# Layers 2 and 3 of a four-layer graph network: TensorE bound to the order of the text, adjacency checks placed behind a chunk's products

## The chip, the cores and the metric

The kernel runs on one core of a Trainium2 chip. The core has five engines that run side by side and wait for one another through semaphores: TensorE (PE in the profile: matrix products and transposes), VectorE (DVE), ScalarE (ACT), GpSimd (POOL) and SyncE (SP, which here only issues transfers). The metric is the time of one execution in microseconds (us) on the device.

## The reference, cut to what matters

Input is x with 8 batches of 2048 nodes and 64 features, and an adjacency matrix of 2048 x 2048 zeros and ones. Four layers follow, each of the form x + layer(relu(layernorm(x))). The change touches the last two.

```python
# layer 2: three steps
v = causal_vars.at[:, intervention_idx].set(intervention_value)
for _ in range(MAX_STEPS):
    effects = jnp.einsum('nm,bmd->bnd', adj_matrix, v)
    h = jnp.concatenate([v, effects], axis=-1)
    h = jax.nn.relu(jnp.einsum('bnk,dk->bnd', h, W1) + b1)
    v = jnp.einsum('bnk,dk->bnd', h, W2) + b2
# layer 3: x, A x and (2 A A - I) x, each with its own weights for every node
w = jnp.einsum('nd,dkio->nkio', embedding, weight)
...
x_g = jnp.einsum('knm,bmc->bnkc', A_stack, x)
out = jnp.einsum('bnki,nkio->bno', x_g, w)
```

The large work is the product of the adjacency matrix with a 2048 x 128 matrix: three times in layer 2 and twice in layer 3, for each pair of batches.

## The kernel before, in words

The function `layers23` (L1438 to L1618) works on one pair of batches at a time (p = 0 to 3), so that 2 x 64 features fill the 128 partitions. The 2048 nodes are cut into 4 chunks of 512 columns (c = 0 to 3) and 16 tiles of 128 (m). The adjacency matrix stays in SBUF as 16 tiles aT.

A "spread" (`spread`, L1510) is one chunk of the product with the adjacency matrix: 32 matmuls of 128x512, two for each m, since the other factor is held as a rounded part `hi` and a rest `lo`. The two parts of a chunk of y are needed by every spread at its four values of m: the last chunk's by m = 12 to 15.

For a pair p the stages are:

- Entering (`enter`, L1519): load a chunk of x2, layer norm (`mean`, `xc`, square, `var`, Ln, Exp, `v`; `kit.norm_steps`, L720), then `moved`: four products `py` with W1e, and from them `hi` (ACT) and `lo`.
- Steps 0, 1 and 2 of layer 2 (L1538): for each chunk a product of v with W1v or Wvc (L1543, called Wv below), a spread, Relu into v (L1545). In steps 0 and 1 `moved` follows: `py` with Wec, `yb` (DVE, L1494), `hi` (ACT, L1495), `lo` (POOL, L1496). In step 2 instead: `pv` with W2 (L1550), `xq` on DVE, the bias sum `bq` on POOL, a store to x3, layer norm, and `turned`: four transposes `tp`, `hi`, `lo`.
- First product of layer 3 (L1565): four spreads into y1, each followed by `turned`.
- Second product and output (L1570): for each chunk a spread into y2, then four blocks of 128 nodes, each with a transpose `px` of x3, its copy `xs` on ACT, twelve products `u` for each half w of the weights (24 in all as the trace counts them), in pairs that use the two halves of the array, DVE's multiplication by the embedding (`pr`) and sums (`fold`), POOL's sums (`ot`) and the store of `out`. The next pair's chunk c - 1 enters at the start of chunk c; its chunk 3 enters after the loop (L1617).

The adjacency matrix must be checked for values other than 0 and 1: `check` (L1461) loads 64 pieces `raw` of 128x512, two ahead of each chunk as written, and DVE counts in each (L1470).

The program is written for a scheduler that orders each engine's instructions by what it expects to be ready; each engine then runs its list in that order. `tc.keep_in_program_order` binds an instruction to the order of the text. Before, only the `u` products are bound, except the first of each twelve:

```python
if kk or h:
    tc.keep_in_program_order(one)
```

Buffers come from pools; tiles of one tag share a number of buffers. `hi` and `lo` have 6 each, so that eight pairs of them can't be held at once; `raw` shares the two buffers of the tag "fold"; `tp`, `py`, `pv`, `px`, `mean` and `var` share two PSUM buffers.

Of the kernel before, what the change touches and what calls it, by code (L numbers as in the profile page):

```python
# [8 lines left out]
FP = mybir.dt.float32  # L9
FR = mybir.dt.float32r  # L10
AF = mybir.ActivationFunctionType
OP = mybir.AluOpType
# [4 lines left out]
P = 128  # L17
B, N, F = 8, 2048, 64
E = 64
NP = B // 2  # L20
NT = N // P
CW = 512
NCW = N // CW
# [8 lines left out]
def cols(c, w=CW):  # L32
    return slice(c * w, (c + 1) * w)
# [588 lines left out]
class Kit:  # L622
# [88 lines left out]
    def mm(self, *args, **kw):  # L711

        one = self.nc.tensor.matmul(*args, **kw)  # L713
        if self.strict:
            self.tc.keep_in_program_order(one)

# [718 lines left out]
        l1.close()  # L1435


def layers23(kit, aT, x2_dram, x3_dram, out):  # L1438

    tc, nc, t = kit.tc, kit.nc, kit.t  # L1440
    mm = nc.tensor.matmul
    ident, ones = kit.ident, kit.ones
    ctx = ExitStack()
    W1v, W1e, W2, Wvc, Wec, cb = kit.W1v, kit.W1e, kit.W2, kit.Wvc, kit.Wec, kit.cb
    b1, b2c, ivc, b1c = kit.b1, kit.b2c, kit.ivc, kit.b1c
    K3, D3 = 3, 16

    fin = ctx.enter_context(tc.tile_pool(name="f_in", bufs=2, reuse_waits="tile"))
    w2 = ctx.enter_context(tc.tile_pool(name="w2f", bufs=1, reuse_waits="tile"))
    sb = ctx.enter_context(tc.tile_pool(name="f_sb", bufs=2, reuse_waits="tile"))  # L1450
    ps = ctx.enter_context(tc.tile_pool(name="f_ps", bufs=2, space=PSUM, reuse_waits="tile"))

    def norm(dst, src):

        mean = ps.tile([P, CW], FP, tag="tp", name="mean")
        var = ps.tile([P, CW], FP, tag="tp", name="var")
        xc = fin.tile([P, CW], FP, tag="ca", name="xc")
        q = fin.tile([P, CW], FP, tag="q", name="q", bufs=1)
        kit.norm(dst, src, mean, var, xc, q)

    def check(n):  # L1461

        for _ in range(n):
            if not todo:
                return
            m, h = todo.pop(0)
            a = sb.tile([P, CW], FP, tag="fold", name="raw")
            nc.sync.dma_start(out=a, in_=t["adjT"][m * P : (m + 1) * P, cols(h)])
            k = 7 + NCW * m + h
            nc.vector.scalar_tensor_tensor(  # L1470
                a, a, 0.5, a, op0=OP.is_gt, op1=OP.not_equal, accum_out=kit.bad[:, k : k + 1]
            )

    todo = [(m, h) for m in range(NT) for h in range(NCW)]

    def parts():
        return (
            sb.tile([P, 4, P], FR, tag="hi", name="hi", bufs=6),
            sb.tile([P, 4, P], FR, tag="lo", name="lo", bufs=6),
        )  # L1480

    def moved(v, c, W, bias):

        py = ps.tile([P, 4, P], FP, tag="tp", name="py")
        for k in range(4):
            m = 4 * c + k
            mm(py[:, k, :], v[:, m * P : (m + 1) * P], W, start=True, stop=True)  # L1487
        hi, lo = parts()
        if bias is None:
            nc.scalar.copy(hi, py)  # L1490
            nc.vector.tensor_tensor(lo, py, hi.bitcast(FP), op=OP.subtract)  # L1491
        else:
            yb = fin.tile([P, 4, P], FP, tag="ca", name="yb")
            nc.vector.tensor_tensor(yb, py, bias[:, None, :].to_broadcast([P, 4, P]), op=OP.add)  # L1494
            nc.scalar.copy(hi, yb)  # L1495
            nc.gpsimd.tensor_tensor(lo, yb, hi.bitcast(FP), op=OP.subtract)  # L1496
        return hi, lo

    def turned(v, c):

        tp = ps.tile([P, 4, P], FP, tag="tp", name="tp")
        for k in range(4):
            m = 4 * c + k
            nc.tensor.transpose(tp[:, k, :], v[:, m * P : (m + 1) * P], ident)
        hi, lo = parts()
        nc.scalar.copy(hi, tp)  # L1506
        nc.vector.tensor_tensor(lo, tp, hi.bitcast(FP), op=OP.subtract)  # L1507
        return hi, lo

    def spread(acc, y, c, start):  # L1510

        for m in range(NT):
            for part in y[m // 4]:
                mm(acc, part[:, m % 4, :], aT[m][:, cols(c)], start=start, stop=m == NT - 1 and part is y[m // 4][1])  # L1514
                start = False

    v = fin.tile([P, N], FP, name="v", bufs=1)

    def enter(p, c):  # L1519

        xp = fin.tile([P, CW], FP, tag="x", name="xp")
        nc.sync.dma_start(out=xp, in_=x2_dram[p, :, cols(c)])
        norm(v[:, cols(c)], xp)
        if c == 0:
            nc.vector.tensor_copy(v[:, 0:1], ivc)
        return moved(v, c, W1e, None)

    y = [enter(0, c) for c in range(NCW)]
    W3 = w2.tile([P, K3, D3 * F], FP, name="W3f")
    for h in range(2):  # L1530
        nc.sync.dma_start(out=W3[half(h)], in_=t["L3_gnn_weight"])
# [2 lines left out]

    nc.vector.tensor_sub(W3[:, 0, :], W3[:, 0, :], W3[:, 2, :])
    nc.vector.tensor_scalar(W3[:, 2, :], W3[:, 2, :], 2.0, None, op0=OP.mult)
    for p in range(NP):
        for step in range(3):  # L1538
            yn = []
            for c in range(NCW):  # L1540
                acc = ps.tile([P, CW], FP, tag="acc", name="acc")
                check(2)
                mm(acc, Wvc if step else W1v, v[:, cols(c)], start=True, stop=False)  # L1543
                spread(acc, y, c, False)
                nc.scalar.activation(v[:, cols(c)], acc, AF.Relu, bias=b1c if step else b1)  # L1545
                if step < 2:
                    yn.append(moved(v, c, Wec, cb))
                    continue
                pv = ps.tile([P, CW], FP, tag="tp", name="pv")
                mm(pv, W2, v[:, cols(c)], start=True, stop=True)  # L1550
                xp = fin.tile([P, CW], FP, tag="x", name="xq")
                nc.sync.dma_start(out=xp, in_=x2_dram[p, :, cols(c)])
                nc.vector.scalar_tensor_tensor(xp, pv, b2c, xp, op0=OP.add, op1=OP.add)
                bq = sb.tile([P, CW], FP, tag="pr", name="bq", bufs=3)
                nc.sync.dma_start(out=bq, in_=kit.bias_dram[:, cols(c)])
                nc.gpsimd.tensor_add(bq, bq, xp)
                nc.sync.dma_start(out=x3_dram[p, :, cols(c)], in_=bq)
                norm(v[:, cols(c)], xp)
                yn.append(turned(v, c))
            y = yn  # L1560


        y1 = sb.tile([P, N], FP, tag="y1", name="y1", bufs=1)
        yn, after = [], []
        for c in range(NCW):  # L1565
            acc = ps.tile([P, CW], FP, tag="acc", name="acc")
            spread(acc, y, c, True)
            nc.scalar.copy(y1[:, cols(c)], acc)
            yn.append(turned(y1, c))
        for c in range(NCW):  # L1570
            acc = ps.tile([P, CW], FP, tag="acc", name="acc")
            spread(acc, yn, c, True)
            y2 = fin.tile([P, CW], FP, tag="ca", name="y2")
            nc.scalar.copy(y2, acc)
            xp = fin.tile([P, CW], FP, tag="x", name="xr")
            nc.sync.dma_start(out=xp, in_=x3_dram[p, :, cols(c)])
            if c > 0 and p + 1 < NP:
                after.append(enter(p + 1, c - 1))
            for k in range(4):
                i = 4 * c + k  # L1580
                ns, ks = slice(i * P, (i + 1) * P), slice(k * P, (k + 1) * P)
                px = ps.tile([P, P], FP, tag="tp", name="px")
                nc.tensor.transpose(px, xp[:, ks], ident)
                xs = sb.tile([P, 2, F], FP, tag="xs", name="xs", bufs=1)
                nc.scalar.copy(xs.rearrange("p h f -> p (h f)"), px)
                pr = []
                for w in range(2):
                    u = [ps.tile([P, 8, F], FP, tag=f"u{h}", name=f"u{h}") for h in range(2)]
                    for kk, src in enumerate((v[:, ns], y1[:, ns], y2[:, ks])):
                        for h in range(2):  # L1590

                            one = mm(  # L1592
                                u[h].rearrange("p d o -> p (d o)"), src[half(h), :], W3[half(h), kk, cols(w)],
                                start=kk == 0, stop=kk == 2,
                            )
                            if kk or h:
                                tc.keep_in_program_order(one)
                    for h in range(2):
                        a = sb.tile([P, 8, F], FP, tag="pr", name="pr", bufs=3)
                        nc.vector.tensor_tensor(  # L1600
# [2 lines left out]
                        if w:  # L1603
                            nc.vector.tensor_add(pr[h], pr[h], a)  # L1604
                        else:
                            pr.append(a)
                fold = sb.tile([P, 2, 4, F], FP, tag="fold", name="fold")
                ot = sb.tile([P, 2, F], FP, tag="ot", name="ot", bufs=1)
                for h in range(2):
# [4 lines left out]
                nc.sync.dma_start(  # L1614
                    out=out[2 * p : 2 * p + 2, ns, :].rearrange("h p f -> p h f"), in_=ot
                )
        y = after + [enter(p + 1, NCW - 1)] if p + 1 < NP else None  # L1617
    ctx.close()  # L1618


# [99 lines left out]
```

## Time and profile before

| | |
|---|---|
| time of three runs | 2155.81, 2156.43, 2158.01 us (median 2156.43) |
| span of the profiled execution | 2160.7 us |
| busy: TensorE, VectorE, ScalarE, GpSimd | 2056.3, 1211.0, 461.1, 297.4 us |
| spread matmuls (L1514) | 960 + 960 + 320 + 320 |
| products `u` (L1592) | 1024 + 512 |
| loads `raw` | 64 of 256 KB, 3.2 us from issue to landing (median) |

A line of the groups has the source line, the engine, the operation, output and inputs by their names in the program, and busy and mean times. The timeline has the start, the length, then the same, and in brackets how long the engine stood idle before and what ended it. The busy time of TensorE counts overlapping matmuls as they lie: spread matmuls last 0.4 us each in the records and start 0.23 us apart.

### The profile page before, as it was taken

The page shows a single profiled execution, that of the slowest core. Times are in us where ns is not written, and L with a number is a line of the kernel's source. Part 1 is how long each engine was busy: PE and PEld are TensorE (multiplying, and loading weights), DVE is VectorE, ACT ScalarE, POOL GpSimd, SP SyncE. Part 2 cuts the span into 40 slices and gives each one's busy share as a digit, 9 for nine tenths or more (in the row PEclk, how much of TensorE's full clock was granted, in tenths as well). Part 3 has the DMA queues.
Part 4 walks back from the last instruction along what each step waited for, and adds up shares of the span by engine and source line. Part 5 has one row for each costly group of instructions (what it writes and reads, how often), then busy time and mean ns, then how long its engine had stood idle before and what let it go on. Part 6 is the DMA issues. An engine that isn't in the chain of part 4 may idle for free.

```text
span 2160.7 us, 23805 instructions
## 1 busy us (share of the span) xinstructions
PE 2056.3 (95%) x9164; PEld 1156.7 (54%) x9164; DVE 1211.0 (56%) x1882; ACT 461.1 (21%) x860; POOL 297.4 (14%) x416
## 2 busy tenths in 40 slices
PE   7999889978999999989999999999999999999997
PEld 4777655523323232226775456665467754576653
DVE  6676488858898988874114652126550246401255
ACT  4322244456111111112121011210111210112100
POOL 0211154411000000000101211102111012111022
PEclk9999899989999999999999999999999999999999
DMA  5666362155011111015100022100030000101000
GB/s 124 182 185 192 104 226 51 37 163 173 28 55 44 54 44 50 30 58 144 35 30 15 24 74 79 35 10 25 21 106 12 33 15 23 37 1 34 12 19 12
DMA packets 86154, 140.26 MB, mean 65 GB/s; under 512 B 33040, under 2 KB 33296, under 8 KB 83792
## 3 DMA queue, kind: packets, MB, share of 16 engines
q1 hardware_dynamic: 67984, 88.05, 13.9%
q0 software_dynamic: 18048, 50.60, 7.8%
q8 instruction: 74, 1.21, 0.2%
q14 instruction: 48, 0.39, 0.1%
HBM read 107.89 MB, written 30.74 MB: 64 GB/s over the span
## 4 chain that ended last, share of the span: by engine, by line
PE 61%; issue 16%; DVE 8%; DMA 6%; POOL 4%; ACT 3%; POOLq 0%; DVEq 0%; SPq 0%; ACTq 0%
PE acc L1514 19%; PE o L713 10%; PE u L1592 7%; PE dn L713 5%; DMA raw<-in_adjT 3%; PE acc L919 2%; PE var L713 2%; PE pgs L1147 2%; PE py L1487 2%; PE mean L713 2%; PE acc L1543 1%; DVE pt L1375 1%; DMA at<-in_adjT 1%; DVE ex L1145 1%; POOL fold L1611 1%
## 5 line engine op out<-in xcount | busy, mean ns | idle before, releaser
L1514 PE MATMUL acc<-aT,hi 128*128 128x512 f32 x960 | 401.4, 418 | 0.0
L1514 PE MATMUL acc<-aT,lo 128*128 128x512 f32 x960 | 388.3, 405 | 0.0
L1592 PE MATMUL u<-W3f,y 64*128 64x512 f32 x1024 | 258.2, 592 | 0.0
L1375 DVE SCALAR_TENSOR_TENSOR pt<-R,wd,aT 128x1024 f32<-128x1024 f32 x192 | 236.9, 1279 | 22.9 <-PE dn L713 10.5
L713 PE MATMUL o<-pt,hS 128*64 128x512 f32 x1024 | 243.5, 602 | 5.7 <-DVE pt L1375 5.2
L1600 DVE TENSOR_TENSOR pr<-u,embf 128x512 f32<-128x512 f32 x256 | 171.4, 688 | 123.0 <-PE u L1592 110.6
L1514 PEld LDWEIGHTS acc<-aT,hi 128*128 128x128 f32 x960 | 180.8, 188 | 62.0 <-issue 23.2
L1514 PEld LDWEIGHTS acc<-aT,lo 128*128 128x128 f32 x960 | 180.7, 188 | 51.2 <-issue 13.6
L1592 PEld LDWEIGHTS u<-W3f,y 64*128 64x128 f32 x1024 | 104.2, 187 | 124.8 <-issue 124.8
L713 PEld LDWEIGHTS o<-pt,hS 128*64 128x64 f32 x1024 | 70.3, 137 | 169.8 <-issue 149.0
L1592 PE MATMUL u<-W3f,v 64*128 64x512 f32 x512 | 146.4, 617 | 0.0
L919 PE MATMUL acc<-at,Y 128*128 128x512 f32 x512 | 134.0, 406 | 1.9 <-DVE ev L928 1.9
L1514 PE MATMUL acc<-aTl,lo 128*128 128x512 f32 x320 | 129.0, 404 | 5.4 <-DVE lo L1491 4.0
L1514 PE MATMUL acc<-aTl,hi 128*128 128x512 f32 x320 | 128.4, 402 | 5.9 <-ACT hi L1495 5.9
L713 PE MATMUL dn<-pt,vd 128*32 128x512 f32 x1024 | 125.3, 598 | 2.7 <-DVE pt L1375 2.7
L1611 POOL TENSOR_TENSOR fold<-fold 128x256 f32<-128x256 f32 x64 | 46.9, 733 | 556.2 <-DVE fold L1610 556.2
L1494 DVE TENSOR_TENSOR yb<-py,cb_f 128x512 f32<-128x512 f32 x32 | 22.1, 690 | 158.2 <-PE py L1487 158.2
L919 PEld LDWEIGHTS acc<-at,Y 128*128 128x128 f32 x512 | 93.5, 191 | 24.3 <-issue 4.2
L1470 DVE SCALAR_TENSOR_TENSOR raw<-raw 128x512 f32<-128x512 f32 x64 | 49.9, 785 | 72.1 <-DMA raw<-in_adjT 71.7
L1604 DVE TENSOR_TENSOR pr<-pr 128x512 f32<-128x512 f32 x128 | 88.1, 688 | 2.2
L1507 DVE TENSOR_TENSOR lo<-tp,hi 128x512 fp32r<-128x512 f32 x32 | 22.1, 692 | 117.5 <-ACT hi L1506 117.5
L1375 DVE SCALAR_TENSOR_TENSOR pt<-R,wd,aTl 128x1024 f32<-128x1024 f32 x64 | 80.0, 1282 | 10.3 <-PE dn L713 7.4
(277 smaller groups left out, 2681.0 us busy)
## 6 DMA issues: line engine op xcount, KB each, us to landing
at<-in_adjT POOLq DMA_DIRECT2D x32, 512.0 KB, 4.7
raw<-in_adjT SPq DMA_DIRECT2D x64, 256.0 KB, 3.2
aT<-in_adjT POOLq DMA_DIRECT2D x12, 1024.0 KB, 6.4
R<-r_dram SPq DMA_DIRECT2D x14, 512.0 KB, 3.7
hi_dram<-hi SPq DMA_DIRECT2D x16, 264.0 KB, 2.6
lo_dram<-lo SPq DMA_DIRECT2D x16, 264.0 KB, 3.5
hhi<-hi_dram POOLq DMA_DIRECT2D x16, 264.0 KB, 3.1
hlo<-lo_dram POOLq DMA_DIRECT2D x16, 264.0 KB, 3.1
```

Source lines behind the costliest of these rows:

```text
L713: one = self.nc.tensor.matmul(*args, **kw)
L919: mm(acc[p], Y[h][:, m, p, :], at[:, k, :], start=m + h == 0, stop=m == NT - 1 and h == 1)
L1147: return lambda: mm(flat(pg), S[:, k, :], flat(mix), start=k == 0, stop=k == NB - 1)
L1375: nc.vector.scalar_tensor_tensor(pt, R[b2], wd[:, m, b2 : b2 + 1], aT[m][:, s].bitcast(FP), op0=OP.max, op1=OP.mult)
L1470: nc.vector.scalar_tensor_tensor(a, a, 0.5, a, op0=OP.is_gt, op1=OP.not_equal, accum_out=kit.bad[:, k : k + 1])
L1487: mm(py[:, k, :], v[:, m * P : (m + 1) * P], W, start=True, stop=True)
L1494: nc.vector.tensor_tensor(yb, py, bias[:, None, :].to_broadcast([P, 4, P]), op=OP.add)
L1514: mm(acc, part[:, m % 4, :], aT[m][:, cols(c)], start=start, stop=m == NT - 1 and part is y[m // 4][1])
L1592: one = mm(u[h].rearrange("p d o -> p (d o)"), src[half(h), :], W3[half(h), kk, cols(w)], start=kk == 0, stop=kk == 2,)
L1600: nc.vector.tensor_tensor(a, u[h], emb[:, i, 8 * w : 8 * w + 8, None].to_broadcast([P, 8, F]), op=OP.mult)
L1604: nc.vector.tensor_add(pr[h], pr[h], a)
L1611: nc.gpsimd.tensor_add(fold[:, :, 0:2, :], fold[:, :, 0:2, :], fold[:, :, 2:4, :])
```

## The change

Layers 2 and 3 are rewritten so that the order of TensorE's instructions is that of the text. All its products and transposes go through `kit.mm` and a new `kit.turn`, which bind them while `kit.strict` is set. So that other chunks' products can still come between, a small class `Weave` keeps a clock in the text: every emitted product adds a stated time (0.47 us for two spread matmuls, 0.93 for Wv, 2.8 for twelve `u`), and each chain of dependent steps is a generator that yields the time until its next product.

```diff
+    def passed(self, us):
+
+        self.now += us
+        for c in list(self.chains):
+            if c[0] <= self.now:
+                self.step(c)
...
+    def carry(c, step, yn):
+        yield 1.4
+        yn[c] = moved(v, c, Wec, cb, None if step else LENT[c])
...
+    def leave(p, c, xp, yn):
+
+        yield 1.4
+        pv = ps.tile([P, CW], FP, tag="tp", name="pv")
...
+        yield 1.8
+        yield from normed(v[:, cols(c)], xp, ("u0", "u1"))
+        yn[c] = turned(v, c, LENT[c])
```

The checks' loads are issued per chunk into the tag "x" (two buffers, shared with the chunks of x), and the counting is bound behind the chunk's spread in the text:

```diff
+                if step < 2:
+                    got = raw(2)
...
                 nc.scalar.activation(v[:, cols(c)], acc, AF.Relu, bias=b1c if step else b1)
                 if step < 2:
-                    yn.append(moved(v, c, Wec, cb))
-                    continue
...
+                    check(got)
+                weave.start(carry(c, step, yn) if step < 2 else leave(p, c, xp, yn))
```

`lo` is computed on DVE, not on POOL. Chunks 2 and 3 of step 0 and step 2 take their `hi` and `lo` from buffers lent by the tags "fold" and "pr". The layer norm uses v itself in place of the buffer `q`, and PSUM buffers of the tags "u0", "u1" or "acc" for `mean` and `var`. The first two chunks of layer 3's first product are interleaved. All four chunks of pair 0 enter before the first spread; chunks 2 and 3 are loaded into `room`, a tile in the place of y1. The entering of a later pair goes on between groups of twelve `u`, and its chunk 3 now enters during the output of chunk 3, in columns of y1, and is copied to v by ACT at the end:

```diff
+                weave.start(enter(c - 1, after, xp, 0.0, ("acc", "acc")))
+                if c == LAST:
+
+                    xp = load(y1[:, cols(0)], x2_dram[p + 1], c)
+                    weave.start(enter(c, after, xp, 2.0, ("acc", "acc"), y1))
...
+        two = [ps.tile([P, CW], FP, tag="acc", name="acc") for c in range(2)]
+        for ms in (range(0, 8), range(8, 12), range(12, NT)):
+            for c in range(2):
+                spread(two[c], y, c, 0 in ms, ms)
...
-        y = after + [enter(p + 1, NCW - 1)] if p + 1 < NP else None
+        if p + 1 < NP:
+            weave.until(lambda: None not in after)
+            nc.scalar.copy(v[:, cols(LAST)], y1[:, cols(1)])
+        y = after
```

## Prediction

> **What bounds the kernel now.** I read the page's totals first, then the times by stage, the waits of TensorE in layers 2 and 3, and the timeline where they fall.
>
> ```profile
> span 2160.7 us, 23805 instructions
> PE 2056.3 (95%) x9164; PEld 1156.7 (54%) x9164; DVE 1211.0 (56%) x1882; ACT 461.1 (21%) x860; POOL 297.4 (14%) x416
> ```
>
> TensorE (PE) is the only engine near full. Layers 2 and 3 run from 957 us to the end. The next view cuts them at the first product of step 0 of each batch pair p = 0, 1, 2, 3; the last stretch ends with the last `u` product.
>
> ```profile
> 957.45:970.97 13.52, 6.49 (x15) 3.34 (x15) 5.12 (x6) 6.19 (x8) 0.53 (x1) 0.62 0.28 88
> 970.97:1274.96 303.99, 297.71 (x1257) 185.66 (x1256) 123.79 (x222) 49.35 (x88) 39.93 (x57) 0.99 0.18 48
> 1274.96:1576.09 301.13, 292.78 (x1233) 183.14 (x1232) 120.68 (x218) 44.38 (x80) 41.87 (x60) 0.99 0.15 42
> 1576.09:1872.59 296.50, 291.42 (x1233) 182.86 (x1232) 115.34 (x203) 44.39 (x80) 41.99 (x60) 0.99 0.12 36
> 1872.59:2149.00 276.41, 275.67 (x1195) 176.18 (x1193) 95.16 (x158) 36.53 (x68) 41.62 (x60) 1.00 0.07 19
> ```
>
> First column is length, second PE's busy time. Pair 3 is 20 to 28 us shorter than the others. Two things are missing in it: the adjacency checks (done by 1617 us) and the entering of a next pair. They are what the change rearranges. Where PE waits:
>
> ```profile
> PE var L713 <- ACT q L727: 10.0, 14, 4.7
> PE acc L1514 <- ACT hi L1495: 5.9, 2, 3.6
> PE acc L1514 <- DVE lo L1491: 4.0, 2, 2.5
> PE acc L1514 <- POOL lo L1496: 1.4, 2, 0.9
> ```
>
> The last three are 11.3 us, in four places (1023, 1284, 1323, 1585 us). The DVE timeline at the third shows why:
>
> ```profile
> 1320.92 0.69 DVE L1470 SCALAR_TENSOR_TENSOR raw<-raw 128x512 f32<-128x512 f32 x1 [2.59 <-DMA raw<-in_adjT]
> ...
> 1325.09 0.69 DVE L1470 SCALAR_TENSOR_TENSOR raw<-raw 128x512 f32<-128x512 f32 x1 [2.44 <-DMA raw<-in_adjT]
> 1325.70 0.08 DVE L1470 DVE_READ_ACCUMULATOR raw<-raw 128x1 f32 x1
> 1325.70 0.69 DVE L1494 TENSOR_TENSOR yb<-py,cb_f 128x512 f32<-128x512 f32 x1
> ```
>
> `py` was finished at 1317.7, but `yb` stands behind three checks, each waiting for its load. `hi`, `lo` and TensorE wait behind `yb`; after that the spread products start 0.43 us apart instead of 0.23. The other loss is in the entering of a next pair, in layer 3 (PE timeline):
>
> ```profile
> 1176.46 1.02 PE L713 MATMUL mean<-xp,avg_f 128*128 128x512 f32 x2
> 1177.41 1.13 PE L1592 MATMUL u<-W3f,v 64*128 64x512 f32 x4
> 1178.92 1.13 PE L713 MATMUL var<-q,avg_f 128*128 128x512 f32 x2 [0.38 <-ACT q L727]
> 1179.98 1.98 PE L1592 MATMUL u<-W3f,y 64*128 64x512 f32 x6
> 1182.40 1.16 PE L1487 MATMUL py<-W1e_f,v 128*128 128x128 f32 x8 [0.44 <-DVE v L1525]
> ```
>
> `var` and `py` come too soon after what they need and wait 0.4 us each. Six `u` records are an odd three products: the pair of halves that otherwise start together (24 records in 5.35 us) is torn.
>
> [...] 8 us of delay for `yb`, ready all the time. [...] 0.43 us spacing after the 3.6 us wait, none after the 2.1 us at 1284. [...] `lo` is 1.29 us on POOL (L1496), 0.69 on DVE (L1491).
>
> **The change, part by part**, from the order in which the changed program issues on each engine; layers 0 and 1 keep theirs.
>
> *Checks.* Two per chunk in steps 0 and 1, on DVE directly before that chunk's `yb`, from two `x` buffers loaded a chunk ahead. The round is two checks (1.6 us), the issues and 3.2 us to landing (9.4 at worst once): under 6 us in a chunk of 9.4. So the four gaps go. Worth, from the stretches: the chunk at 1018.45 took 14.5 us instead of 9.45 (5.0); the one at 1317 6.6 too much; 1284.26 to 1286.81 2.1 too much; 1585.39 to 1592.94 4.4. Sum 18.1; it agrees with 11.3 us of waits and about 6.8 us of slow products. The DVE work per chunk (two checks, `yb`, `lo` from POOL: 3 us) lies beside 9.4 us of PE.
>
> *Entering in layer 3.* Chunks 1 to 3 take 27.59, 27.41 and 27.41 us with an entering, a chunk of pair 3 without takes 22.38. 82.4 - 67.1 = 15.3 us per pair; the products themselves (`mean` 0.95, `var` 0.97, `py` 1.0) need 2.9 x 3 = 8.8. In the new order they stand between whole groups of twelve `u`: `var` 5.35 us after `mean`, `py` 5.6 us after `var`. DVE has xc before the group, v before the fold: Exp is ready about 2.5 us after `var`, v at some 4. No wait, so 6.5 us per pair return: 19.5 for three.
>
> *Chunk 3 carries two enterings*, the second in `y1`'s columns; its 2.9 us of products come from step 0's first chunks, where they are now: no gain. A new wait: the second `py` needs the PSUM buffer of the first, which DVE's `lo` frees late, since v of the second waits for Exp, behind `xs`, behind POOL's `ot`. Counting on: `lo` ends 20.6 us into the chunk, PE is there at 19.3. Loss 1.4 per pair, 4.2 in all (bounds 0 and 10).
>
> *SP's queue in layer 3.* The loads of the entering stand between the stores of `out`, which wait for POOL's `ot` (some 6 us behind the last `u` of a block of rows). Each load is issued before the last store of its chunk, and the next chunk's 7.5 us of spreads cover the 3 us to landing: nothing. The load into `y1` waits for chunk 0's `u` only, two chunks ahead of its use: nothing.
>
> *First product of layer 3.* `tp` of the last chunk stands two spread products (0.47 us) ahead of the products that read it; `hi` ends 1.34 and `lo` 2.06 us after `tp` begins (trace at 1113). Before, 18 products lay between. Loss 0.9 x 4 = 3.6 (0.5 to 1.5 each).
>
> *Steps 0 to 2.* `py` and `pv` come two spread products after `Wv`. Today they come directly after it and wait for Relu (chunk 9.46). Apart they cost one more change from fp32 to fp32r, 0.40 us (0.63 against 0.23 after a 512-wide fp32 product). A chunk then is 7.47 + 0.86 + 1.06 = 9.39, the last step's 11.6 against 11.76. Gain 2, bounds -5 and +5. `lo` on DVE, lent buffers, ACT's three copies of 0.6 us: off PE's path; nothing, hidden under spreads.
>
> *Start of layer 2.* All four enterings now come before the first spread. On SP, chunks 2 and 3 (`room`) are behind two raw loads, which wait for xc of chunks 0 and 1 (961.1 and 961.8); W3f follows, held to 968.4 by layer 1's last store as today. DVE has the W3f subtraction before v of chunk 3; both loads land 6.1 to 8.2 us after issue, so 977, subtraction 1.2, v 0.7, `py` 1 to 2: first product at 981 instead of 970.97. But today's first chunks then hold three enterings (8.8 us and 0.4 of waits). Plus a slow clock in the first spreads: loss 1 (bounds: gain 4 if W3f lands early, loss 5).
>
> Sum against the span: 18.1 + 19.5 - 4.2 - 3.6 + 2 - 1 = 30.8. The profiled span, 2160.7, is 4.3 above the median 2156.43 of the runs: 2156.4 - 30.8 = **2125.6 us**.
>
> **Rivals.** (A) The bound order stalls in the entering: at 9 places v or Exp arrives 2 us late behind folds and POOL. For it: ACT's `xs` waits 302 us in all for POOL's `ot`. Against: v stands early in DVE's order. The 19.5 us vanish: 2145. (B) The start is better than I count and the new waits are absorbed: 30.8 + 5 + 4.2 + 3.6 = 44 us, 2113. (C) Slower: TensorE, no longer free to take another product, waits at each of the 48 `py`/`pv` behind Relu. The slot is 1.33 us after the last spread (0.86 + 0.47), Relu is ready at 1.0 today. If Relu comes x later than the slot at all 48, the cost is 48x; from x = 0.64 it exceeds the gain; at 0.8 it is 38 us: 2164. It needs one extra ACT operation of 0.69 us in front of each Relu; ACT is only a sixth busy, and its order has one only in the last step, so x of this size is improbable. (D) No effect: the scheduler's order would have to be what it was; the issue order says it isn't.
>
> **Numbers.** Main case 0.66, B 0.10, A 0.14, C 0.07, within 0.2% 0.03 (gains and losses cancel). 0.2% (4.3 us) is about what a measurement of this kernel can tell from no change. Range: the main case's bounds taken together are 14 us less (start 5, chunk 3 4.2, `tp` 1.6, steps 3) and 19 more (4, 5.8, 2.4, 7), 2112 to 2145; with some slack for the two gains, which takes in B and the middle of A: 2110 to 2146. Faster 0.90, same 0.03, slower 0.07.
>
> **What would show it.** Right: pairs 0 to 2 near 287 us and pair 3 near 274; no raw wait of a DVE `yb`; chunks 1 and 2 of layer 3 near 25.5 us, chunk 3 near 30; `tp` of the last chunk followed by 0.9 us of PE waiting. Wrong: PE waits for Relu in every chunk (C), for v in layer 3 (A), or a first spread after 985.

## The result, and the profile after

The changed kernel takes 2120.9 us, the median of four runs (2116.35 to 2124.13), where the kernel before took 2156.1 (2155.47 to 2158.01): ratio 0.9834, 95% interval [0.9809, 0.9858]. Run again in the last group of the experiments it took 2118.45 us against 2158.72, ratio 0.9811 [0.9784, 0.9838]. The forecast was 2125.6, a gain of 30.8 us; measured are 35 and 40. The page of the profiled execution:

```profile
span 2115.9 us, 23671 instructions
...
PE 2025.5 (96%) x9164; PEld 1158.4 (55%) x9164; DVE 1221.2 (58%) x1914; ACT 461.7 (22%) x863; POOL 258.5 (12%) x384
```

TensorE has the same 9164 products and is busy 31 us less, and the span is 45 us shorter: products stand closer, and there is less idle time between them. The times by stage, cut at the same places as before (first `mean` of layer 2, then the first product of step 0 of each pair, to the last `u`):

```profile
954.11:980.38 26.27, 15.07 (x50) 7.71 (x49) 12.70 (x17) 12.74 (x19) 0.53 (x1) 0.81 0.52 125
980.38:1265.34 284.96, 284.21 (x1235) 183.69 (x1233) 113.77 (x205) 44.47 (x80) 29.76 (x49) 0.99 0.13 37
1265.34:1548.88 283.54, 282.79 (x1235) 182.99 (x1233) 116.95 (x209) 44.66 (x81) 32.14 (x52) 1.00 0.13 38
1548.88:1832.47 283.59, 282.83 (x1234) 183.01 (x1233) 116.96 (x209) 44.66 (x81) 32.15 (x52) 1.00 0.13 38
1832.47:2104.00 271.53, 270.90 (x1186) 177.23 (x1184) 110.16 (x198) 34.88 (x66) 32.14 (x52) 1.00 0.11 33
```

Pairs 0 to 2 lost 19.0, 17.6 and 12.9 us, pair 3 about 5, and the stretch ahead of them grew from 13.5 to 26.3. The three pairs with checks or an entering are now equal to 1.4 us, where they were 303.99, 301.13 and 296.50. The waits of TensorE after:

```profile
PE var L713 <- ACT v L1550: 4.2, 2, 3.8
PE mean L713 <- DMA room<-xd: 3.5, 1, 3.5
PE py L713 <- DVE v L1556: 3.5, 2, 3.3
...
PE acc L713 <- DVE lo L1541: 1.1, 4, 0.3
PE acc L713 <- ACT hi L1540: 1.0, 4, 0.2
...
PE py L713 <- DVE lo L1530: 0.7, 3, 0.2
```

The waits of `acc` for `hi` and `lo` of up to 3.6 us and the `var` waits of the later enterings are gone. What is left is the start of layer 2 (the first three lines, 11 us in all), `tp` of the last chunk (four times 0.5), the second `py` of the doubled entering (three times 0.2) and, at the very end, 2.4 us that the kernel before has too. On DVE, `yb` waits for `py` alone now, and no line of DVE's waits names a raw load (before: 48 waits, 71.7 us):

```profile
DVE yb L1527 <- PE py L713: 191.9, 32, 10.2
```

Executions differ ahead of the change: layers 0 and 1 stand in the same order in both kernels, yet layer 2's first `mean` is at 957.45 us in the profiled execution before, at 954.11 after, and at 957.93 in another of the changed kernel. So the experiments are also compared by the time from that `mean` to the start of the last `u`, "the two layers" below: 1191.0 us before, 1149.2 and 1147.1 after.

### The profile page after: what moved, and what is told of

The parts are those of the page before. It is cut to its first block, busy times and chain, and to the rows that moved or that the text cites. A ratio compares the mean times of both kernels' runs of the same rounds, so it can differ in the third digit from the quotient of the medians.

```text
span 2115.9 us, 23671 instructions
## 1 busy us (share of the span) xinstructions
PE 2025.5 (96%) x9164; PEld 1158.4 (55%) x9164; DVE 1221.2 (58%) x1914; ACT 461.7 (22%) x863; POOL 258.5 (12%) x384
## 4 chain that ended last, share of the span: by engine, by line
PE 48%; issue 35%; DVE 6%; POOL 5%; DMA 3%; ACT 2%; POOLq 0%; SPq 0%; DVEq 0%; ACTq 0%
PE acc L713 27%; PE u L713 5%; PE acc L925 2%; PE pgs L1153 2%; PE py L713 2%; POOL fold L1701 1%; DVE ex L1151 1%; PE var L713 1%; PE mean L713 1%; POOL ot L1702 1%; POOL ot L1703 1%; DMA at<-in_adjT 1%; POOL mix L1152 1%; PE tp L719 1%; PE pv L713 1%
## 5 line engine op out<-in xcount | busy, mean ns | idle before, releaser
L713 PE MATMUL acc<-aT,hi 128*128 128x512 f32 x960 | 420.4, 438 | 0.0
L713 PE MATMUL acc<-aT,lo 128*128 128x512 f32 x960 | 380.1, 396 | 0.0
L713 PE MATMUL u<-W3f,y 64*128 64x512 f32 x1024 | 241.0, 589 | 0.0
L713 PEld LDWEIGHTS u<-W3f,y 64*128 64x128 f32 x1024 | 99.2, 187 | 120.6 <-issue 120.6
L713 PE MATMUL u<-W3f,v 64*128 64x512 f32 x512 | 138.8, 619 | 0.0
L1153 PE MATMUL pgs<-mix,S 128*128 128x512 f32 x128 | 69.8, 635 | 13.1 <-POOL mix L1152 12.2
```

The source lines that it names most:

```text
L1153: return lambda: mm(flat(pg), S[:, k, :], flat(mix), start=k == 0, stop=k == NB - 1)
```

## The experiments

Each was timed against the kernel before on the same chip, in three groups on three chips; between groups the ratios are to be compared, not the times.

| kernel | time, us | ratio to before, 95% interval | the two layers, us |
|---|---|---|---|
| before | 2156 to 2160 | 1 | 1191.0 |
| before, checks bound | 2145.7 | 0.9936 [0.9916, 0.9956] | 1173.9 |
| before, first `u` bound | 2137.4 | 0.9901 [0.9880, 0.9922] | 1166.0 |
| before, both | 2120.5 | 0.9816 [0.9794, 0.9838] | 1152.0 |
| changed | 2120.9; 2118.5 | 0.9834; 0.9811 | 1149.2; 1147.1 |
| changed, checks not bound | 2161.2 | 1.0014 [1.0003, 1.0026] | 1189.4 |
| changed, `py` right behind `Wv` | 2124.0 | 0.9829 [0.9812, 0.9846] | 1155.9 |
| changed, `py` still later | 2118.2 | 0.9818 [0.9795, 0.9841] | 1151.1 |
| changed, `lo` on POOL | 2119.1 | 0.9819 [0.9794, 0.9845] | 1149.1 |
| changed, start repaired | 2112.0 | 0.9781 [0.9762, 0.9800] | 1145.1 |
| changed, three chunks | 2112.9 | 0.9784 [0.9765, 0.9803] | 1144.5 |
| changed, start and three | 2108.9 | 0.9773 [0.9750, 0.9795] | 1141.0 |
| changed, start, three, `hi` | 2102.6 | 0.9746 [0.9724, 0.9769] | 1136.0 |

The profiled executions differ in one more thing. In four of them (changed, the first of the two; `py` still later; `lo` on POOL; three chunks) the first products of step 0 ran at half clock behind a wait (in the changed kernel the granted clock is 0.50 from 980.5 to 983.9 us), and the first chunk took 9.9 us instead of 8.3. Their last column holds 1.6 us for that, which the other rows of the changed kernel do not have. At full clock the changed kernel has 1147.1.

**1. The checks alone, in the kernel before.**

```diff
-                check(2)
+                got = raw(2) if step < 2 else []      # into two buffers of tag x
                 mm(acc, Wvc if step else W1v, ...)
                 spread(acc, y, c, False)
                 nc.scalar.activation(v[:, cols(c)], acc, AF.Relu, ...)
+                check(got)                            # each bound in DVE's order
```

> The kernel before with one part of the change alone: the raw blocks are loaded into the two x buffers at the head of a chunk and checked on DVE, bound in order, behind that chunk's Relu; everything else stays as before. My account of the sum: the four gaps of steps 0 and 1 go, 18.1 us, and nothing else moves: 2138 us (2135 to 2141), chunks of layer 3 with an entering still 27.4 to 27.6 us. Rival (the gaps close only because TensorE's order is bound; moving the checks alone lets DVE or SP hold yb elsewhere): less than 5 us of gain, 2151 or more, and waits of yb for raw remain.

2145.7 us, above the expected 2135 to 2141; by the ratio, 0.9936, it is 9.5 to 18.1 us less, with the forecast at the edge of the interval. The profile is sharper: the two layers are 17.1 us shorter, all chunks of steps 0 and 1 without an entering are 9.39 to 9.45 us (four of them 13.84, 15.80, 10.05 and 9.67 before), and layer 3 keeps its lengths, 30.70, 35.16 and 34.97 us from the first `u` of a chunk to that of the next. DVE still waits twice for raw, 3.0 us in all, and nobody stands behind it. The gaps were an effect of the checks, and TensorE's order need not be bound for them to go. Which part of this edit does it isn't separated: it moves the checks behind the spread, binds them there, and gives their loads other buffers.

**2. The first product of `u` bound, in the kernel before.**

```diff
-                            if kk or h:
-                                tc.keep_in_program_order(one)
+                            tc.keep_in_program_order(one)
```

> The kernel before with one line changed: the first of the twelve u products of a group is bound like the eleven others, so that no other product can stand inside a group; the scheduler then puts mean, var and py of an entering between the spread products of the next y2 chunk instead of between u products. My account: the entering's loss of 6.5 us per pair comes from torn pairs of u and the two 0.4 us waits, so it goes though nothing else of TensorE's order is bound: 19.5 us, 2137 us (2133 to 2141). Rival (the entering costs what its products cost wherever they stand, or needs the timed chains): 2153 or more, with 27.4 us per chunk.

2137.4 us, as forecast, by removing one condition. In the order of issue `mean`, `var` and `py` of an entering have moved out of the `u` groups into the next chunk's spreads: 32 spreads, `mean`, 7 spreads, `var`, 10 spreads, `py`. All `u` then come in groups of 24 that take 5.35 us each. From one chunk's first `u` to the next it is 32.73 us where it was 35.16 and 34.97, and 29.93 without an entering: an entering now costs 2.8 us, its products. The two layers are 25.0 us shorter, the time 21.4. Some 3 us of the 25.0 are not the enterings: the checks fell elsewhere too, and two chunks with gaps shrank (13.84 to 11.01 us, 15.80 to 14.38).

**3. Both together.**

> The kernel before with both of these parts (checks bound behind Relu, first u product bound) and no timed chain, no lent buffer, lo still on POOL. My account: the two gains add, 18.1 + 19.5 = 37.6 us: 2118.5 us (2114 to 2124), as fast as the whole change, whose remaining parts then are worth nothing in sum. Rival (the shorter chunks of steps 0 to 2 that the changed kernel shows, 9.20 against 9.46 us, are a gain of their own that only the bound order gives, and nothing is lost against it): 2128 or more; a chunk of steps 0 and 1 is 9.46 us here in both accounts.

2120.5 us: equal to the whole change, within what the timing can tell. In the two layers it is 39.0 us shorter: 17.1 from the first part, 21.9 from the second on top of it. From 985 us to the last `u`, TensorE waits for nothing but 0.3 us in one `pv`, with `lo` on POOL and no timed chain. A chunk of steps 0 and 1 is 9.45 us here, the changed kernel's 9.21; much of what the changed kernel gains in its steps it gives back elsewhere.

**4. The changed kernel, checks not bound.**

```diff
-            one = nc.vector.scalar_tensor_tensor(
+            nc.vector.scalar_tensor_tensor(
                 a, a, 0.5, a, op0=OP.is_gt, op1=OP.not_equal, ...
             )
-            tc.keep_in_program_order(one)
```

> The changed kernel with the checks not bound on DVE (one line less); loads and buffers as in it. The scheduler then lets checks run ahead: seven in front of the first yb of pair 0, and those of later pairs into layer 3, in front of DVE's reads of u. My account (what counts is what stands behind a check that waits for its load): DVE waits for raw return and hold yb and u; gaps of 2 to 10 us in every pair with checks, 2145 us (2133 to 2175). Rival (with TensorE's order bound and PSUM buffers enough, DVE's order no longer matters): 2121 us, within 4.

2161.2 us: without this one line the whole gain is gone. One half of my account was wrong: the checks that run ahead of `yb` (six in a row before the first) cost nothing, chunks of steps 0 and 1 stay 9.23 us. DVE's order shows why the gaps do not return: all 16 checks of a pair are done before the second `yb` of its step 0, whose result is wanted only some chunks later. None stands before the `yb` of a last chunk, whose `hi` and `lo` the very next spread reads, so that this run does not test what such a check would cost in the changed kernel. The loss is in layer 3. DVE timeline of this kernel in chunk 3 of pair 0, and TensorE's below it:

```profile
1250.18 0.69 DVE L1506 SCALAR_TENSOR_TENSOR raw<-raw 128x512 f32<-128x512 f32 x1 [1.80 <-DMA raw<-in_adjT]
...
1253.90 0.69 DVE L1506 SCALAR_TENSOR_TENSOR raw<-raw 128x512 f32<-128x512 f32 x1 [2.41 <-DMA raw<-in_adjT]
...
1257.57 0.68 DVE L1529 TENSOR_TENSOR lo<-py,hi 128x512 fp32r<-128x512 f32 x1
```

```profile
1258.31 2.08 PE L713 MATMUL py<-W1e_f,y 128*128 128x128 f32 x8 [6.03 <-DVE lo L1529]
```

Checks of the next pair stand among DVE's reads of `u` and in front of `lo`; most of them wait for their loads; the second `py` wants the PSUM buffer that `lo` reads and waits 6 us. The products behind that wait are slow as well (twelve `u` in 4.5 us, not 2.8), and some `u` and `px` wait 0.4 to 1 us for DVE and ACT. From its first `u`, chunk 3 takes 41.5 us instead of 28.1, 40 us over three pairs.

**5. `py` and `pv` at three places.** The delay of `carry` and `leave` is changed; the checks and the enterings keep their places, and in the traces the other engines keep nearly all of their order (in the later one 36 of ACT's 863 operations and 6 of DVE's 1914 stand elsewhere).

```diff
     def carry(c, step, yn):
-        yield 1.4
+        yield 0.9     # the other kernel: 2.4; both the same in leave
```

> The changed kernel with py and pv issued directly behind the next chunk's Wv product, as the kernel before does, instead of two spread products later (both delays 0.9 instead of 1.4). It tells why a chunk of steps 0 and 1 is 9.21 us in the changed kernel and 9.45 before. My account: directly behind Wv the weight load of py waits for v from Relu, which shows as longer spacing of Wv and py and not as idle time of TensorE; two products later v is there. Then this kernel has chunks of 9.4 to 9.5 us and a last step near 11.7, about 12 us more: 2133 us (2127 to 2137). Rival (the position is free, the gain comes from binding or from lo on DVE; one change from fp32 to fp32r less per chunk is saved here, 0.40 us): chunks of 8.8 us, 48 x 0.40 = 19 us less, 2102.

> The changed kernel with py and pv two further spread products and more behind Wv (both delays 2.4 instead of 1.4). My account (v is ready before the weight load in the changed kernel already, so nothing more is to be had): chunks stay 9.21 us, last steps 11.31, the time equal within 3 us, save that tp of chunk 3 comes another 1 us later and the stall ahead of the first product of layer 3 grows by about 1 us per pair, 4 us more: 2125. Rival (some waiting for v is still left in the 9.21): chunks of 9.0 or less, 6 us less or more.

Right behind `Wv`: chunks of 9.39 and 9.47 us, in the last step 11.51. Two spread products later, as in the changed kernel: 9.21 and 11.31. Eight products later: 9.21 and 11.33. The two layers are 6.7 us longer in the first, where I expected 12. Part of the difference is the half clock at the start, which this execution was spared: against the changed kernel at full clock (1147.1) it is 8.8. The rest is mostly the last step, which lost less (11.12 and 11.51 against 10.89 and 11.31). The timing, 0.9829, doesn't resolve that. The chunks tell it: behind `Wv` the chunk is longer though one change from fp32 to fp32r less is paid (0.40 us: the first two spread products behind `Wv` start 0.63 us apart, not 0.23). In the changed kernel a chunk is `Wv` 0.46, two spreads 0.87, `py` 0.81, thirty spreads 7.07; right behind `Wv` it is `Wv` 0.94, `py` 0.91, thirty-two spreads 7.52. The start of such a chunk in both, right behind `Wv` first:

```profile
1016.94 1.02 PE L713 MATMUL acc<-v,Wvc_f 128*128 128x512 f32 x2
1017.88 1.16 PE L713 MATMUL py<-Wec_f,v 128*128 128x128 f32 x8
1018.79 0.48 PE L713 MATMUL acc<-aT,hi 128*128 128x512 f32 x1
```

```profile
1273.74 1.02 PE L713 MATMUL acc<-v,W1v_f 128*128 128x512 f32 x2
1274.20 0.80 PE L713 MATMUL acc<-aT,hi 128*128 128x512 f32 x1
...
1275.07 1.06 PE L713 MATMUL py<-Wec_f,v 128*128 128x128 f32 x8
1275.88 0.48 PE L713 MATMUL acc<-aT,hi 128*128 128x512 f32 x1
```

The 0.48 us more between `Wv` and `py` is where the weight load of `py` waits for Relu. The waits of the weight loads in the kernel with `py` right behind `Wv`:

```profile
PEld py L713 <- ACT v L1633: 25.1, 32, 0.8
...
PEld pv L713 <- ACT v L1633: 10.4, 16, 0.8
```

All 48 are there; the kernel before has them too (22.8 and 10.6 us), the changed one has none. TensorE's own waits don't list them. In the changed kernel the weight load of `py` begins at 1274.84 us, while the spread product before it runs (1274.83 to 1275.23) and 0.23 us ahead of `py` itself, and `py` shows nothing of the wait: 0.81 us to the next start instead of 0.91. The later place cost what was expected in kind, not in size: the stall behind `tp` grew by 0.5 us a pair, not 1.

**6. `lo` of steps 0 and 1 on POOL again.**

```diff
-        nc.vector.tensor_tensor(lo, py, hi.bitcast(FP), op=OP.subtract)
+        (nc.vector if bias is None else nc.gpsimd).tensor_tensor(lo, py, ...)
```

> The changed kernel with lo of steps 0 and 1 back on POOL (1.29 us there against 0.69 on DVE). My account: lo is wanted a whole step later, so its engine costs TensorE nothing: equal to the changed kernel within 2 us, chunks 9.21 us. Rival (lo on DVE is part of why the chunks are shorter): chunks of 9.3 to 9.5 us, 3 to 9 us more.

0.9819 and 1149.1 us against 0.9811 and 1147.1 to 1149.2; chunks 9.21. That part of the change is worth nothing that these runs show.

**7. The start repaired.**

```diff
-                    got = raw(2)
+                    with tc.issue_after(last.ins):    # last: the fourth entering load
+                        got = raw(2)
...
-    nc.vector.tensor_sub(W3[:, 0, :], ...)
-    nc.vector.tensor_scalar(W3[:, 2, :], ...)
+    nc.gpsimd.tensor_sub(W3[:, 0, :], ...)
+    nc.gpsimd.tensor_scalar(W3[:, 2, :], ...)
```

> The changed kernel with the start of layer 2 repaired: the first raw loads are queued on SP behind the four entering loads, and the two operations on W3f are on POOL instead of DVE. My account: mean of chunk 2 no longer waits 3.5 us for its room load, nor v of chunk 3 behind the W3f subtraction (3.3 us); the first Wv comes about 22 us after the first mean instead of 26.3, and less of the first chunk runs at half clock: 4 to 6 us less, 2116 us. Rival (the loads into room wait for memory that layer 1 frees late, whatever stands ahead of them): Wv still 25 us or more after the first mean, 2120 or more.

2112.0 us; its interval overlaps the changed kernel's, and in the two layers it is 2.0 us shorter than the changed kernel at full clock. The wait of the last `py` for v fell from 3.3 to 0.9 us, as expected: W3f stood in front of that v. But `mean` of chunk 2 still waits 4.0 us for its load, and the first `Wv` is 24.2 us after the first `mean`, not 22: the raw loads were not what held `room`. Half of the account is wrong, and the rival right on that half.

**8. Three chunks interleaved at the start of layer 3.**

```diff
         for ms in (range(0, 8), range(8, 12), range(12, NT)):
-            for c in range(2):
+            for c in range(3):
+                if len(two) == c:
+                    two.append(ps.tile([P, CW], FP, tag="u0", name="acc"))
                 spread(two[c], y, c, 0 in ms, ms)
...
-        for c in range(2, NCW):
+        for c in range(3, NCW):
```

> The changed kernel with three chunks of y1 instead of two interleaved at the start of layer 3 (the third accumulates in a buffer of tag u0), so that some 30 spread products instead of 2 to 4 lie between tp of chunk 3 and the first product that reads it. My account: the stall of 1.0 us per pair goes, 4 us in all, 2117 us, and the groups of 16 spreads behind tp take 3.8 us instead of 4.84. Rival (the stall moves: the third chunk's copy and tp come late, or its buffer is not free): same as the changed kernel, 2121.

From the last `Wv` to the first `u` it is 53.96 us instead of 55.00 in all four pairs, and both `acc` waits for `hi` and `lo` are gone: 1.04 a pair, 4.2 in all. The time is 2112.9 us, a difference that the timing alone doesn't resolve.

**9. Both repairs, and then a third.**

> Both repairs of the changed kernel together, start of layer 2 and three interleaved chunks. My account: they touch different stages and add: 8 to 10 us less than the changed kernel, 2112 us (2109 to 2115), faster than both kernels of the case. Rival (either repair fails or is given back later): 2117 or more.

The repairs add: 1141.0 us for the two layers, 6.1 less than the changed kernel at full clock, where they gave 2.0 and 4.2 apart, and 2108.9. SP's waits at the start of layer 2 in this kernel:

```profile
SPq L1610 <- DVE pt L1381: 18.3, 1, 18.3
SPq L1610 <- DVE xr L1407: 11.9, 1, 11.9
```

The second line is what holds `room`: it lies in memory that layer 1's last addition, `xr`, frees. So the last kernel takes other memory:

```diff
-        xp = ... if c < 2 else room[:, cols(c)]
+        xp = ... if c < 2 else sb.tile([P, CW], FP, tag="hi", name="room", bufs=6)
```

> Both repairs, and chunks 2 and 3 of the first entering are loaded into two buffers of tag hi instead of room, which lies in memory that layer 1's last addition on DVE frees (SP waited 11.9 us for it). My account: the mean of chunk 2 then waits less than 1.5 us instead of 3.9 (the next limit is v of chunks 0 and 1), the first Wv comes 21 to 23 us after the first mean instead of 24.1, 2 us less than with both repairs alone: 2107 to 2111 us, 0.976 of the kernel before. Rival (the second load waits for other memory of layer 1 all the same): no difference to both repairs.

TensorE's waits in it, from 940 us on:

```profile
PE var L713 <- ACT v L1550: 4.1, 2, 3.8
...
PE py L713 <- DVE v L1556: 1.4, 3, 0.9
```

No wait for `room` is left. The first `Wv` is 19.0 us after the first `mean` (21 to 23 expected), and the kernel takes 2102.6 us, ratio 0.9746, against 2118.45 and 0.9811 for the changed kernel in the same group: the intervals don't touch, it beats both kernels.

## Why the prediction was right, term by term

The direction and the main two mechanisms were right, and the forecast was 4 to 10 us short. That it was no further off is in part luck, since two terms missed in opposite directions: steps 0 to 2 gave 11.4 us more than the sum had, far beyond their bound, and the start lost 4.1 us more. Measured on the profiles of before and after, in the two layers:

| term | forecast | measured | by |
|---|---|---|---|
| gaps of the checks | +18.1 | +17.1 | experiment 1 |
| enterings, chunk 3's wait included | +15.3 | +19.4 | pairs, below |
| `tp` | -3.6 | -4.2 | experiment 8 |
| steps 0 to 2 | +2 | +13.4 | pairs, experiment 5 |
| start of layer 2 | -1 | -5.1 | first `mean` to third `Wv`, 40.3 before, 45.4 after |
| sum | 30.8 | 40.6 | 41.8 in all; 1.2 not placed |

**Checks.** As the prediction put it: with the checks placed and bound behind each chunk's spread the gaps go (experiment 1). Left unbound, the scheduler puts them into layer 3, where they cost more than the gaps did (experiment 4).

**Enterings.** From the first `u` of layer 3 to the next pair's first `Wv` it is 128.2 us before and 124.2 after with one entering more; the entering that left step 0 takes 2.4 us out of its first chunks (20.21 to 17.61, less 0.2 for the shorter chunk). So 6.5 a pair, 19.4 in three. I had 6.5 as the gain ahead of a loss of 1.4 in chunk 3. That chunk does take 29.18 us against 25.09 for one with a single entering, 1.4 over the sum of two. But the step that gave 1.4 failed: the wait for the PSUM buffer is 0.2 us, since `lo` ends earlier than counted. What takes the time is the order itself, TensorE timeline after:

```profile
1239.99 1.13 PE L713 MATMUL mean<-y,avg_f 128*128 128x512 f32 x2
1241.05 1.13 PE L713 MATMUL u<-W3f,v 64*128 64x512 f32 x4
1242.01 1.88 PE L713 MATMUL u<-W3f,y 64*128 64x512 f32 x8
1243.83 1.12 PE L713 MATMUL var<-v,avg_f 128*128 128x512 f32 x2
...
1255.86 1.16 PE L713 MATMUL py<-W1e_f,y 128*128 128x128 f32 x8 [0.22 <-DVE lo L1530]
```

The second entering's products stand in the middle of three blocks of rows. Two such blocks take 5.55 us instead of 5.35, the one with the second `py` 5.85, and each of the three products 0.1 more from its start to the next: that is most of the 1.4. That loss had the right size and the wrong cause; the gain of the other chunks was 1.4 a pair more than the sum had.

**Steps 0 to 2**, the term that made the forecast short. The prediction had the mechanism (directly behind `Wv`, `py` waits for Relu) and the price of the place (one more change to fp32r, 0.40), and then added pieces to 9.39 where 9.21 came. The failed piece is `py` itself: the sum has 1.06 us for it and the change behind it. After, it is 0.81 to the next start and the change 0.09 (0.32 us from the first spread product to the second instead of 0.23), 0.90 in all, since its weights are loaded early (0.23 us ahead of it and with no wait for v, experiment 5). The sum's own pieces, 0.07 us a chunk and 0.16 in the last step, also come to some 4 to 5 us in four pairs, not to the 2 that it states. From the third `Wv` of pair 2 to its first `u` it is 143.90 us before and 141.79 after, with `tp`'s 1.04 in it; with the second chunk's 0.2 that is 3.35 a pair, 13.4 in four. Experiment 5 gives 8.8 us of the 13.4 to the place of `py` and `pv`. The rest is in the last step, where the weight loads of `var` wait for ACT before (25.6 us in all with those of the enterings); in the changed kernel, behind the start of layer 2, none does, and `var` takes 0.45 us to the next start instead of 0.56. So the same thing seems to happen to `var`, but no run shows it apart. My bound of +5 was too low.

**Start of layer 2.** The loss was at my bound of 5, not at 1. v of chunk 3 did stand behind W3f, which I had counted (a wait of 3.3 us, 0.9 in experiment 7). What I had not seen is that `room` stands in memory which layer 1 frees last, so that `mean` of chunk 2 waits 3.5 us (experiment 9). The half clock after the waits takes another 1.6 us of the first chunk in this execution.

**`tp`.** 1.04 a pair against 0.9, as described.

**The rivals.** (C) is refuted by the place, not only by its size: the kernel before is the one in which 48 products stand behind Relu (33 us of waits of their weight loads), and the change takes them out of it. (A) did not come: TensorE waits for no v or Exp in layer 3. (B) had the right direction by the wrong terms. What the prediction did not consider is that two small edits of the kernel before would be enough (experiment 3): timed chains, lent buffers and the doubled entering are worth 3 to 5 us together in the two layers, which the timing doesn't resolve, and only the repairs make more of them.

## What to carry to other kernels

DVE ran its list in order here: `yb` stood some 8 us behind checks that waited for their loads. Where that is so, ask for each unbound instruction what could come to stand behind it while it waits for a load: one line that bound the checks decided 40 us here, in layer 3 and not in the steps they were written in. A product that is bound in all but its first instruction can be torn there; binding that one too gave 21 us here. And a chunk that grows with no listed wait of TensorE is looked up among the waits of its weight loads: here `py`, whose stationary operand was ready when it stood two products later, made each chunk of steps 0 and 1 some 0.2 us shorter.

## What the runs showed that was not expected

In these traces a weight load that waits for Relu shows as a later start behind the product ahead of it, not as idle time of TensorE: from `Wv` to the next start it is 0.94 us instead of 0.46, and the busy time counts it as work (in the kernel before, 1.91 us of the 1.91 from `Wv` at 1059.42 us to the next spread product).

Whether a pause cost the clock depended on more than its length. Behind the last `py` of the start, whose wait for v differed a little in each execution of the changed kernel and its variants, the first products ran at full speed after 2.78 and 2.92 us and at half speed for some 3.4 us after 2.93, 3.08, 3.28 and 3.48; the first chunk took 8.3 and 9.9 us. In the kernel before, a shorter pause was followed by half speed too, with products 0.43 us apart instead of 0.23 (granted clock 0.50 from 1588.5 to 1591.9 us):

```profile
1588.92 0.79 PE L1514 MATMUL acc<-aTl,lo 128*128 128x512 f32 x1 [2.50 <-DVE lo L1491]
1589.51 0.63 PE L1514 MATMUL acc<-aTl,hi 128*128 128x512 f32 x1
1589.93 0.63 PE L1514 MATMUL acc<-aTl,lo 128*128 128x512 f32 x1
```

The prediction compared only the wait of 3.6 us and the one at 1284, which lasts 1.53 us in the trace (2.1 is how late the products came); the waits in between show more. Two pauses of 2.92 and 2.93 us differ, and one of 2.50 us costs the clock where one of 2.92 doesn't. Nor does the clock fall at one point of the pause: in the kernel before at 1588.5 us, 0.4 us ahead of the product that ends the 2.50 us, in the changed kernel at 980.5, 1.1 us behind the start of the `py` that ends the 3.28 us. What else decided it, no run shows.
